# A four-layer kernel on one core: its last phase in another order, and layernorm statistics aggregated by fours

## The chip, the core and the metric

The kernel runs on one core of a Trainium2 chip. The core has five engines with instruction streams of their own: TensorE (PE) for matmuls, VectorE (DVE), ScalarE (ACT) and GpSimd (POOL) for elementwise work, and SyncE (SP), which here issues the DMAs. They wait for one another through semaphores. PE's matmuls write to PSUM, and the other engines empty PSUM into SBUF. The metric is the time on the device in microseconds (us), as the median of several runs.

## The reference

The input is x of 4 batches with 1024 tokens of 256 numbers, all float32. Four layers follow one another, each added to its input:

```python
x = x + attention(layernorm(x))   # one head, causal softmax, no output product
x = x + mix(layernorm(x))
x = x + state(layernorm(x))
x = x + mix(layernorm(x))         # the same weights as above

def mix(x):                       # x_prev: the token before, zero ahead of the first
    xr = mu_r * x + (1 - mu_r) * x_prev
    xk = mu_k * x + (1 - mu_k) * x_prev
    return sigmoid(xr @ W_r.T) * (square(relu(xk @ W_k.T)) @ W_v.T)

def state(x):
    xn = (x - mean) / sqrt(var + 1e-5) * ln_g + ln_b
    x_proj, z = split(xn @ W_in.T + b_in, 2)
    z = silu(z)
    y = conv(x_proj @ W_B.T * mean(dt)) @ W_C.T + D_skip * x_proj
    return (y * z) @ W_out.T + b_out + x
```

The convolution runs along the tokens of a batch, with 16 channels, each with a kernel of averaged powers of its decay.

## The kernel before, in words

The tokens of a batch are worked in two halves of 512; half j is half j % 2 of batch j // 2, so there are eight, 0 to 7. The names of tiles carry the layer and the half: a is the attention's normalization, f the first mix, h the state layer, g the second mix, whose result is the output. A tile with features on the partitions and tokens along the row is 128x512, and a half has two of them (e = 0, 1); a tile with tokens on the partitions is 128x256, and a half has four of them.

**The work of one half in a layer.** `normalized` (L584) makes the statistics of four tiles of rows: bn_stats (L622) and bn_aggr (L623) of each on DVE, then the variance ve (L648), its power −1/2 rs on POOL (L661), the shift mrs (L670), and the normalized rows xn on DVE (L676, L688) or ACT. For the second mix some halves are done with sums on ACT instead. `by_dram` (L731) turns them: rows_ is written to memory and read back as blocks_ by four DMAs, all on SP's queue, and DVE transposes the blocks (L750) into hT. The mix shifts it into xk and xr (L974 on ACT, L977 on DVE). Then come, on PE, keys (p.gks, L858, or pk, L793 where a half is done alone), gates pr (L928, the sigmoid of it is r) and values pv (L928); ka (L1038, L1047) is the squared relu of the keys, r is multiplied by the values on DVE (L1095), and the sum with x is made on POOL (L1101).

**Products by seven.** For a whole batch, `seven_products` (L840) makes a product of 2x2 blocks with seven block products instead of eight. The units on PE are called p1, p2, p6, p5, p7, p4, p3. Sums T1 to T4 of the input's halves are made ahead (`stream_sums`, L832) on POOL or DVE; three of the intermediate products are copied out of PSUM as u (L783 on ACT, L784 on DVE); and DVE combines these with the products held in PSUM (L905, L907) into the four results c11, c22, c21, c12. The keys of mix 2 (gks), the gates of the state layer (zs), its skip path (ss) and the attention's queries (qs) of most batches go this way.

**The state layer.** z is the gate, skip the skip path, `mix_states` (L1942) makes py = states times W_C on PE, adds it to skip (L1961 on DVE) and multiplies z by that (L1965, on POOL or DVE). `state_outputs` (L1982) is the product pyo with W_out, and DVE adds it to x (L1989). `convolve` (L1856) needs the inputs of all four batches, so the layer has a meeting point: gates and skip paths can come before or after it, outputs only after it.

**What sets the order.** A planner, `Order` (L54), gets the work as units for PE in the order in which the program calls them, and as operations with one or more ways to do each (engine and cost in us, for instance POOL 1.05 or DVE). It computes when each is due, places them in a list schedule, with 20 plans and some rounds for each, and emits the plan that ends first by its own costs. PE's units keep the order of the calls, except that of the next few one that is ready may go ahead; which engine makes an operation, and when, is the planner's choice and depends on all costs. PSUM is a ring of four bank buffers and two pairs.

**The last phase** (from L2131) is a list of calls written out by hand: `more_gates(n)` issues the next n pieces of gates and skip paths of the state layer, `mix_states(b)` one batch's mixing, `outputs(j)` (L2127) a half's state output and the preparation of its second mix, `both(mix2.gates, j)` the gate of the second mix, `keys_of_batch(b)` with `advance(keys, n)` n of a batch's seven key units, `both(mix2.values, j)` the values.

Of the kernel before, what the change touches and what calls it, by code (L numbers as in the profile page):

```python
# [14 lines left out]
AF = mybir.ActivationFunctionType  # L15
ALU = mybir.AluOpType
# [13 lines left out]
HALF = 512  # L30
# [329 lines left out]
def dve(n):  # L360
    return 0.02 + n / 850


def act(n):
    return 0.22 + n * 0.72e-3
# [3 lines left out]
def hybrid_kernel(  # L369
# [34 lines left out]
    nc = tc.nc  # L404
    E = mybir.EngineType
    ctx.enter_context(tc.manual_schedule(engines={E.PE, E.Activation, E.DVE, E.Pool, E.SP}))
    o = Order()
# [120 lines left out]
    for j in range(4, 2 * NB):  # L528
        b, h = divmod(j, 2)
# [23 lines left out]
    for i in range(NB * NT):  # L553
        j = i // NH
# [29 lines left out]
    def normalized(  # L584
        key, b, h, needs, dst, names, second=False, by_hand=False, spans=((0, NH),),
        by_scalar=False,
# [11 lines left out]
        st = lazy(lambda: tiny(f"st_{key}", NH, 6))  # L598
        mv = lazy(lambda: tiny(f"mv_{key}", NH, 2))
# [20 lines left out]

        def stats(n):
            nc.vector.bn_stats(st()[:, n, :], row(n))  # L622
            nc.vector.bn_aggr(mv()[:, n, :], st()[:, n, :])  # L623

        def sums(n):
            nc.scalar.activation(
# [66 lines left out]
        if by_scalar:  # L693
            for n in range(NH):
                o.op(f"{key}.su{n}", [needs[n]], ("ACT", act(D) + 0.11, partial(sums, n)))
            o.op(f"{key}.me", [f"{key}.su{n}" for n in range(NH)], ("POOL", 0.2, means))
            for n in range(NH):
                o.op(f"{key}.st{n}", [f"{key}.me"], ("ACT", act(D) + 0.11, partial(squares, n)))
            variances_of = lambda n0, n1: by_sums()
            shifts_of = lambda n0, n1: shifts_by_sums()  # L700
        else:
            for n in range(NH):
                o.op(f"{key}.st{n}", [needs[n]], ("DVE", 0.53, partial(stats, n)))
            variances_of, shifts_of = variances, shifts
        for n0, n1 in spans:
            span = "" if n1 - n0 == NH else f"{n0}"
            some = range(n0, n1)
            o.op(
                f"{key}.ve{span}", [f"{key}.st{n}" for n in some],
                ("DVE+port", 0.08 * k, partial(variances_of, n0, n1)),  # L710
            )
            o.op(
                f"{key}.rs{span}", [f"{key}.ve{span}"],
                ("POOL", 0.4 + 0.62 * k, partial(powers, n0, n1)),
            )
            o.op(
                f"{key}.mrs{span}", [f"{key}.rs{span}"],
                ("DVE+port", 0.08 * k, partial(shifts_of, n0, n1)),
            )
            for n in some:  # L720
                o.op(
                    f"{key}.xn{n}", [f"{key}.mrs{span}"],
                    ("DVE+port", dve(D), partial(on_vector_by_sums if by_scalar else on_vector, n)),
                    ("ACT", act(D) + 0.1, partial(on_scalar, n)),
                )
# [89 lines left out]
    def stream_sums(key, src, needs):  # L815

        t = [lazy(lambda k=k: cols(f"T{k}_{key}")) for k in range(KC)]

        def b(c, h):
            return src(h)[:, c, :]  # L820

        def sums(k):
            return t[(k - 1) // 2]()[:, (k - 1) % 2, :]

        for k, plus, minus in (
            (1, lambda: b(0, 1), lambda: b(0, 0)),
            (3, lambda: b(1, 1), lambda: b(0, 1)),
            (2, lambda: b(1, 1), lambda: sums(1)),
            (4, lambda: b(1, 0), lambda: sums(2)),
        ):  # L830
            def emit(engine, k=k, plus=plus, minus=minus):
                engine.tensor_sub(sums(k), plus(), minus())  # L832

            o.op(
                f"{key}.T{k}", needs + ([f"{key}.T{k - 1}"] if k in (2, 4) else []),
                ("POOL", 1.05, partial(emit, nc.gpsimd)), ("DVE+port", dve(HALF), partial(emit, nc.vector)),
            )
        return sums

# [103 lines left out]

    class Mix:
        def __init__(self, tag, needs, last):
            self.tag, self.needs, self.last = tag, needs, last
# [52 lines left out]
        def keys(self, j, e):  # L1001
            key = f"{self.tag}{j}"
            if e == 0:
                self.ka[j] = lazy(lambda: cols(f"ka_{key}"))
            ka = self.ka[j]
            pk = project_columns(
                f"{key}.pk{e}", w_fk, e, self.xk[j], [f"{key}.xk{c}" for c in range(KC)] + ["w_f"]
            )
            o.op(
                f"{key}.relu{e}", [f"{key}.pk{e}"],  # L1010
                ("ACT", act(HALF), lambda: nc.scalar.activation(ka()[:, e, :], pk(), AF.Relu)),
                ("DVE", dve(HALF), lambda: nc.vector.tensor_scalar_max(ka()[:, e, :], pk(), 0.0)),
                frees="bank",
            )
            o.op(
                f"{key}.ka{e}", [f"{key}.relu{e}"],
                ("POOL", 1.05, lambda: nc.gpsimd.tensor_mul(ka()[:, e, :], ka()[:, e, :], ka()[:, e, :])),
                ("ACT", act(HALF), lambda: nc.scalar.square(ka()[:, e, :], ka()[:, e, :])),
            )

        def keys_of_batch(self, b):

            js = (2 * b, 2 * b + 1)
            key = f"{self.tag}ks{b}"
            there = [f"{self.tag}{j}.xk{c}" for j in js for c in range(KC)]
            for j in js:
                self.ka[j] = lazy(lambda j=j: cols(f"ka_{self.tag}{j}"))
            ka, xk = [self.ka[j] for j in js], [self.xk[j] for j in js]

            def src(h):  # L1030
                return xk[h]()

            def by_scalar(t):
                nc.scalar.activation(t(), t(), AF.Relu)
                nc.scalar.square(t(), t())

            def by_vector(t):
                nc.vector.scalar_tensor_tensor(t(), t(), 0.0, t(), ALU.max, ALU.mult)  # L1038

            T = stream_sums(key, src, there)  # L1040
            o.op(f"{self.tag}{js[0]}.ka1", [f"{key}.c21"], ("none", 0.0, lambda: None), lag=0.0)
            out = lambda e, h: ka[h]()[:, e, :]

            def direct(e, h, p):
                def emit():
                    nc.scalar.activation(out(e, h), p(), AF.Relu)
                    nc.scalar.square(out(e, h), out(e, h))  # L1047

                return (("ACT", 2 * act(HALF), emit),)

            for e, h in ((0, 0), (1, 1), (0, 1)):
                t = lambda e=e, h=h: ka[h]()[:, e, :]
                o.op(
                    f"{self.tag}{js[h]}.ka{e}", [f"{key}.c{e + 1}{h + 1}"],
                    ("ACT", 2 * act(HALF), partial(by_scalar, t)),
                    ("DVE+port", dve(HALF), partial(by_vector, t)),
                )
            return seven_products(
                key, key, fk_block, lambda k: fk_sums[:, k - 1, :], src, T,
                added(out), direct, ["fk_sums", "w_f"], there,  # L1060
            )

# [879 lines left out]
    def mix_states(b):  # L1942
# [25 lines left out]
        for h in range(2):  # L1968
            j = 2 * b + h
            for e in range(KC):  # L1970
                o.op(
                    f"g{e}.{j}", [f"pm{b}", f"ss{b}.c{e + 1}{h + 1}"],
                    ("DVE", dve(HALF) + 0.03, partial(grown, j, e)),
                    frees="bank",
                )
                o.op(
                    f"y{e}.{j}", [f"g{e}.{j}", f"z{e}.{j}"],
                    ("POOL", 1.05, partial(gated, nc.gpsimd, j, e)),
                    ("DVE+port", dve(HALF), partial(gated, nc.vector, j, e)),
                )  # L1980

# [18 lines left out]
    def both(unit, j):  # L2000
        unit(j, 0)
        unit(j, 1)
# [115 lines left out]
    def more_gates(n):  # L2118

        for _ in range(n):  # L2120
            next(all_gates)

    def advance(chain, n):
        for _ in range(n):
            next(chain)

    def outputs(j):  # L2127
        both(state_outputs, j)
        mix2.prepare(j)
# [37 lines left out]
    mix_states(0)  # L2167
    more_gates(8)
    outputs(0)
    more_gates(5)  # L2170
    mix_states(1)
    outputs(1)
    more_gates(4)
    outputs(2)
    more_gates(4)
    mix_states(2)
    outputs(3)
    more_gates(3)
    keys = mix2.keys_of_batch(0)
    both(mix2.gates, 0)  # L2180
    outputs(4)
    advance(keys, 2)
    outputs(5)
    advance(keys, 2)
    more_gates(3)
    advance(keys, 3)
    both(mix2.gates, 1)
    mix_states(3)
    both(mix2.values, 0)
    both(mix2.values, 1)  # L2190
    outputs(6)
    keys = mix2.keys_of_batch(1)
    both(mix2.gates, 2)
    outputs(7)
    advance(keys, 7)
    both(mix2.gates, 3)
    both(mix2.values, 2)
    keys = mix2.keys_of_batch(2)
# [66 lines left out]
```

## Time and profile before

| | |
|---|---|
| median of 3 runs | 464.14 us (464.13 to 464.68) |
| the profiled execution | 464.18 us |
| its span, from the first to the last instruction | 462.4 us |
| mean granted TensorE clock | 1.000 |
| instructions in the span | 6630 |
| DMA | 69.44 MB, 149 GB/s over the span |

The span is cut into 40 slices on the page of the profile, and each digit is the busy share in tenths:

```profile
PE   8999999999999999999999999999999999999996
DVE  4898697989989888788989977425689989998852
ACT  3322334453284453554335755523467887743452
POOL 3001002303032412332221568512255216336240
```

A slice is 11.6 us. The attention and the first mix fill the first 24 slices or so, the meeting point of the state layer lies at slices 24 to 27, where DVE and POOL have little to do, and the outputs and the second mix fill the rest. A row of the timeline gives the start, the duration, the engine and line, the operation with its output and inputs, and the idle time before it with what ended it. Ends of matmuls are modelled: the distance from one group's start to the next one's is the better measure.

### The profile page before, as it was taken

What the parts mean: (1) busy time and instruction counts of PE and PEld (TensorE: products, weight loads), DVE (VectorE), ACT (ScalarE), POOL (GpSimd) and SP (SyncE); (2) the same over time, 40 slices, a digit from 0 to 9 for tenths busy, and PEclk for the clock granted to TensorE, in tenths of its full rate; (3) what the DMA queues carried; (4) which work ended last, traced back from release to release, by engine and by line L of the source; (5) the groups of instructions that cost most, each with busy time, mean ns of one, the idle gap of its engine ahead of it and who ended that gap; (6) DMA issues with size and microseconds to landing.
All of it is one profiled execution on the core that took longest, in us unless ns stands there. A gap on an engine that the chain in (4) does not pass through costs nothing.

```text
span 462.4 us, 6630 instructions
## 1 busy us (share of the span) xinstructions
PE 454.6 (98%) x2052; PEld 311.4 (67%) x2052; DVE 370.7 (80%) x914; ACT 227.0 (49%) x473; POOL 139.4 (30%) x145
## 2 busy tenths in 40 slices
PE   8999999999999999999999999999999999999996
PEld 5665776667786767776678774473565857686675
DVE  4898697989989888788989977425689989998852
ACT  3322334453284453554335755523467887743452
POOL 3001002303032412332221568512255216336240
PEclk9999999999999999999999999999999999999999
DMA  8067958684358641428784869503014042604522
GB/s 236 27 170 209 272 143 236 169 252 151 101 160 213 184 138 51 137 87 256 226 261 128 276 220 276 213 15 90 13 63 121 0 143 86 215 14 135 178 75 68
DMA packets 84915, 69.44 MB, mean 150 GB/s; under 512 B 20160, under 2 KB 82576, under 8 KB 84880
## 3 DMA queue, kind: packets, MB, share of 16 engines
q1 hardware_dynamic: 84064, 68.76, 50.2%
q8 instruction: 16, 0.26, 0.2%
q10 hardware_dynamic: 816, 0.26, 0.2%
q14 instruction: 19, 0.16, 0.1%
HBM read 40.54 MB, written 28.45 MB: 149 GB/s over the span
## 4 chain that ended last, share of the span: by engine, by line
PE 84%; DVE 10%; POOL 3%; issue 1%; SPq 1%; DMA 1%; ACT 0%; DVEq 0%; POOLq 0%
PE po L1655 14%; PE sc L1550 13%; PE pv L1522 6%; PE held_zs L858 3%; PE held_ss L858 3%; PE held_qs L858 2%; PE held_gks L858 2%; PE pc L1862 2%; PE dust L1339 1%; DVE T_gks L832 1%; DVE xr_g L977 1%; DVE xk_g L977 1%; POOL x L1101 1%; PE pp_a0.pq L793 1%; PE pp_g6.pk L793 1%
## 5 line engine op out<-in xcount | busy, mean ns | idle before, releaser
L1655 PE MATMUL po<-v,prT 128*128 128x256 f32 x288 | 67.6, 380 | 0.0
L1550 PE MATMUL sc<-xa,q 128*128 128x512 f32 (+3 forms) x192 | 66.9, 486 | 0.0
L1655 PEld LDWEIGHTS po<-v,prT 128*128 128x128 f32 x288 | 54.2, 189 | 11.6 <-issue 3.1
L1571 ACT ACTIVATE pr<-pr,nmx 128x128 f32<-128x128 f32 (+7 forms) x32 | 24.7, 773 | 69.7 <-DVE pr L1566 57.1
L1550 PEld LDWEIGHTS sc<-xa,q 128*128 128x128 f32 x192 | 34.8, 190 | 24.3 <-issue 20.1
L1522 PE MATMUL pv<-wv,xa 128*128 128x257 f32 x128 | 32.7, 380 | 0.0
L1101 POOL TENSOR_TENSOR x<-x,r_f 128x512 f32<-128x512 f32 x16 | 20.8, 1298 | 35.7 <-DVE r_f L1095 33.8
L1522 PEld LDWEIGHTS pv<-wv,xa 128*128 128x128 f32 x128 | 23.9, 191 | 8.4 <-issue 4.1
L1608 DVE STREAM_TRANSPOSE prT<-pblocks 128x384 f32<-128x384 f32 (+7 forms) x30 | 24.0, 798 | 4.8 <-DMA pblocks<-exps 4.8
L661 POOL TENSOR_TENSOR rs_h<-ve_h,minus_half 128x8 f32<-128x8 f32 x8 | 13.2, 1646 | 47.9 <-DVE ve_h L650 47.9
L1566 DVE TENSOR_SCALAR_CACHE_REDUCE pr<-sc,v 128x128 f32<-128x128 f32 (+7 forms) x32 | 26.2, 818 | 1.1
L661 POOL TENSOR_TENSOR rs_a<-ve_a,minus_half 128x4 f32<-128x4 f32 x7 | 7.4, 1060 | 62.8 <-DVE ve_a L648 52.9
L1101 POOL TENSOR_TENSOR x<-x,r_g 128x512 f32<-128x512 f32 x14 | 20.1, 1446 | 16.8 <-DVE r_g L1095 16.8
L1699 POOL TENSOR_TENSOR x<-x,bout_r 128x512 f32<-128x512 f32 x16 | 20.7, 1302 | 13.3 <-ACT x L1692 9.8
L1692 ACT ACTIVATE x<-x,mrs_h,rs 128x256 f32<-128x256 f32 x32 | 17.2, 588 | 6.5 <-DVE rs L1703 6.5
L1965 POOL TENSOR_TENSOR z<-z,skip 128x512 f32<-128x512 f32 x11 | 15.0, 1384 | 17.4 <-DVE skip L1961 17.3
L661 POOL TENSOR_TENSOR rs_f<-ve_f,minus_half 128x4 f32<-128x4 f32 x8 | 8.1, 1016 | 39.2 <-DVE ve_f L648 34.1
L1664 DVE SCALAR_TENSOR_TENSOR x<-po,rsm,x 128x256 f32<-128x256 f32 x32 | 14.9, 467 | 5.4 <-PE po L1655 5.3
L622 DVE BATCH_NORM_STATS2 st_a<-x 128x6 f32<-128x256 f32 x32 | 13.0, 407 | 3.0 <-DMA x<-in_L_attn_a_X_dram 3.0
L974 ACT ACTIVATE xk_g<-hT_g,muk 128x512 f32<-128x512 f32 x16 | 11.0, 713 | 8.4 <-DVE hT_g L750 8.4
L1532 DVE TENSOR_TENSOR v<-pv,bv_r 128x257 f32<-128x257 f32 x32 | 13.2, 413 | 2.2 <-PE pv L1522 1.8
L977 DVE SCALAR_TENSOR_TENSOR xr_g<-hT_g,mur,xr_g 128x512 f32<-128x512 f32 x16 | 14.4, 920 | 0.5 <-ACT xr_g L974 0.5
(478 smaller groups left out, 1070.3 us busy)
## 6 DMA issues: line engine op xcount, KB each, us to landing
hk<-r_dram SPq DMA_DIRECT2D x16, 512.0 KB, 6.6
rows_g<-xn_g SPq DMA_DIRECT2D x8, 512.0 KB, 3.0
blocks_g<-rows_g SPq DMA_DIRECT2D x32, 128.0 KB, 2.7
x<-in_L_attn_a_X_dram SPq DMA_DIRECT2D x7, 512.0 KB, 5.1
rows_f<-xn_f SPq DMA_DIRECT2D x7, 512.0 KB, 3.5
blocks_f<-rows_f SPq DMA_DIRECT2D x28, 128.0 KB, 2.7
rows_h<-xn_h SPq DMA_DIRECT2D x7, 512.0 KB, 3.3
blocks_h<-rows_h SPq DMA_DIRECT2D x28, 128.0 KB, 2.9
```

Of the source, the lines that this page charges most:

```text
L661: nc.gpsimd.tensor_tensor(rs()[:, :k].rearrange("p k n -> p (k n)"), ve()[:, :k].rearrange("p k n -> p (k n)"), minus_half[:, : k * NH], A ...
L858: lambda: nc.tensor.matmul(dst(), lhsT=w(), rhs=data(), start=first, stop=True, skip_group_check=True),
L977: nc.vector.scalar_tensor_tensor(t()[:, c, :], hT()[:, c, :HALF], mu1[:, c : c + 1], t()[:, c, :], ALU.mult, ALU.add,)
L1101: nc.gpsimd.tensor_add(xg, xg, r()[:, ts(g, 2), :])
L1522: nc.tensor.matmul(pv()[:, : D + 1], lhsT=xaj()[:, c, ts(n, P)], rhs=wv[:, c, :], start=(c == 0), stop=(c == KC - 1),)
L1550: nc.tensor.matmul(sc()[:, k * HALF : k * HALF + w], lhsT=qh()[:, c, ts(n, P)], rhs=keys[k]()[:, c, :w], start=(c == 0), stop=(c == KC - 1),)
L1566: nc.vector.tensor_scalar(dst, src, v[2 * b + h]()[:, n, D : D + 1], None, ALU.add, ALU.min, accum_out=nmx(),)
L1571: nc.scalar.activation(p()[:, :nk], p()[:, :nk], AF.Exp, bias=nmx(), scale=-1.0, accum_out=sm())
L1608: nc.vector.transpose(dst()[:, : NH * width].rearrange("p (k m a) -> p k m a", m=NH, a=GRP), blocks().rearrange("p m (k a) -> p k m a", a= ...
L1655: nc.tensor.matmul(po()[:, :D], lhsT=src()[:, ts(n, P)], rhs=v[2 * b + n // NH]()[:, n % NH, :D], start=(n == 0), stop=(n == t),)
L1692: nc.scalar.activation(xt, xt, AF.Identity, bias=mrs()[:, 0, n : n + 1], scale=rs1()[:, n : n + 1])
L1699: nc.gpsimd.tensor_add(xg, xg, bout_r.unsqueeze(1).to_broadcast([P, 2, D]))
```

## The change

It has four parts.

- The operation on a tile's statistics held bn_stats and bn_aggr; now bn_stats alone is in it, and a new operation, `ag`, does the aggregates of a group of rows (four, or the part of them that a span names) when all their statistics are there.
- The planner's cost of a POOL multiply or sum of 128x512 goes from 1.05 to 1.25 in three places: the sums T, the squares ka of a half done alone, and the z products.
- The two ways of a squared relu of the keys of a batch move to a helper, `squares`. The instructions are the same, the costs given to the planner are 1.13 and 0.03 more.
- The calls of the last phase stand in another order: outputs of halves 1 to 3 and the mixing of batches 1 and 2 come between fewer pieces of the gates; the key units of batch 0 alternate with the remaining gates one by one; outputs(5) comes after these; the mixing of batch 3 comes after the gates of half 2; values(1) and outputs(6), outputs(7) come in between the key units of batch 1.

```diff
@@ normalized
         def stats(n):
             nc.vector.bn_stats(st()[:, n, :], row(n))
-            nc.vector.bn_aggr(mv()[:, n, :], st()[:, n, :])
+
+        def gather(n0, n1):
+            for n in range(n0, n1):
+                nc.vector.bn_aggr(mv()[:, n, :], st()[:, n, :])
...
             for n in range(NH):
-                o.op(f"{key}.st{n}", [needs[n]], ("DVE", 0.53, partial(stats, n)))
+                o.op(f"{key}.st{n}", [needs[n]], ("DVE", 0.36, partial(stats, n)))
...
+            made = [f"{key}.st{n}" for n in some]
+            if not by_scalar:
+                o.op(
+                    f"{key}.ag{span}", made,
+                    ("DVE", 0.06 + 0.1 * (n1 - n0), partial(gather, n0, n1)),
+                )
+                made = [f"{key}.ag{span}"]
             o.op(
-                f"{key}.ve{span}", [f"{key}.st{n}" for n in some],
+                f"{key}.ve{span}", made,
...
@@ stream_sums
-                ("POOL", 1.05, partial(emit, nc.gpsimd)), ("DVE+port", dve(HALF), partial(emit, nc.vector)),
+                ("POOL", 1.25, partial(emit, nc.gpsimd)), ("DVE+port", dve(HALF), partial(emit, nc.vector)),
@@ Mix
+    def squares(dst, src, port=""):
+
+        def by_scalar():
+            nc.scalar.activation(dst(), src(), AF.Relu)
+            nc.scalar.square(dst(), dst())
+
+        def by_vector():
+            nc.vector.scalar_tensor_tensor(dst(), src(), 0.0, src(), ALU.max, ALU.mult)
+
+        return ("ACT", 1.13, by_scalar), ("DVE" + port, dve(HALF) + 0.03, by_vector)
...
@@ Mix.keys
-                ("POOL", 1.05, lambda: nc.gpsimd.tensor_mul(ka()[:, e, :], ka()[:, e, :], ka()[:, e, :])),
+                ("POOL", 1.25, lambda: nc.gpsimd.tensor_mul(ka()[:, e, :], ka()[:, e, :], ka()[:, e, :])),
@@ mix_states
-                    ("POOL", 1.05, partial(gated, nc.gpsimd, j, e)),
+                    ("POOL", 1.25, partial(gated, nc.gpsimd, j, e)),
@@ the last phase, from L2167
     mix_states(0)
     more_gates(8)
     outputs(0)
-    more_gates(5)
+    more_gates(2)
     mix_states(1)
+    more_gates(2)
     outputs(1)
-    more_gates(4)
+    more_gates(1)
     outputs(2)
-    more_gates(4)
+    more_gates(2)
+    outputs(3)
+    more_gates(2)
     mix_states(2)
-    outputs(3)
-    more_gates(3)
     keys = mix2.keys_of_batch(0)
     both(mix2.gates, 0)
+    advance(keys, 2)
+    more_gates(2)
     outputs(4)
-    advance(keys, 2)
+    for _ in range(5):
+        advance(keys, 1)
+        more_gates(1)
+    both(mix2.gates, 1)
     outputs(5)
-    advance(keys, 2)
     more_gates(3)
-    advance(keys, 3)
-    both(mix2.gates, 1)
-    mix_states(3)
     both(mix2.values, 0)
-    both(mix2.values, 1)
-    outputs(6)
     keys = mix2.keys_of_batch(1)
     both(mix2.gates, 2)
+    mix_states(3)
+    both(mix2.values, 1)
+    advance(keys, 4)
+    outputs(6)
+    advance(keys, 3)
     outputs(7)
-    advance(keys, 7)
     both(mix2.gates, 3)
     both(mix2.values, 2)
```

More of the change, by code (lines that the diff above doesn't have):

```diff
@@ L1031, in src @@
                 return xk[h]()
[L1033 to L1038, printed above, removed]
             T = stream_sums(key, src, there)
@@ L1044, in direct @@
             def direct(e, h, p):
[L1045 to L1049, printed above, removed]
+                return squares(lambda: out(e, h), p)[:1]
             for e, h in ((0, 0), (1, 1), (0, 1)):
@@ L1054, in keys_of_batch @@
                     f"{self.tag}{js[h]}.ka{e}", [f"{key}.c{e + 1}{h + 1}"],
-                    ("ACT", 2 * act(HALF), partial(by_scalar, t)),
-                    ("DVE+port", dve(HALF), partial(by_vector, t)),
+                    *squares(t, t, "+port"),
                 )
```

## The prediction, written before the changed kernel was run

> **What bounds the kernel now.** I read the busy table first, then what TensorE waits for, then busy time by stretch of the last phase, then the timelines of the stretches with a wait.
>
> ```profile
> PE 454.6 (98%) x2052; PEld 311.4 (67%) x2052; DVE 370.7 (80%) x914; ACT 227.0 (49%) x473; POOL 139.4 (30%) x145
> ```
>
> TensorE (PE) is busy for 98% of the span of 462.4 us. Matmuls are the same 1077 before and after, in another order, so the time changes only by what TensorE waits. Its waits (total, times, longest, in us):
>
> ```profile
> PE dust L1339 <- DVE idle L446: 1.2, 1, 1.2
> PE pr_g4.pv L928 <- ACT ka_g L1047: 0.9, 1, 0.9
> PE held_gks L858 <- DVE u_gks L784: 0.9, 1, 0.9
> PE held_zs L858 <- DVE z L907: 0.6, 1, 0.6
> PE pt_h7.T L775 <- DVE xn_h L676: 0.3, 1, 0.3
> ```
>
> The first is the start and isn't touched. The other four lie where the change works. I size them from start to start: sixteen 256-wide matmuls take 3.45 us (g2.pv starts at 408.49, the next group at 411.94), so 0.216 each, and a 512-wide one 0.43. In the timelines (start, duration, instruction, idle time before it):
>
> ```profile
> 324.14 1.02 PE L858 MATMUL held_ss<-xnT,wk 128*128 128x512 f32 x2
> 324.95 0.75 DVE L907 SCALAR_TENSOR_TENSOR z<-held_zs,b_all,u_zs 128x512 f32<-128x512 f32 x1
> 325.75 1.13 PE L858 MATMUL held_zs<-T_zs,w_in 128*128 128x512 f32 x2 [0.59 <-DVE z L907]
> ```
>
> Two 512-wide matmuls end at 324.14 + 0.86 = 325.0 and the next starts at 325.75: 0.75 lost to a buffer that DVE empties late.
>
> ```profile
> 422.36 1.89 PE L928 MATMUL pr_g5.pr<-w_r,xr_g 128*128 128x256 f32 x8
> 422.76 1.27 POOL L1101 TENSOR_TENSOR x<-x,r_g 128x512 f32<-128x512 f32 x1
> 422.82 1.23 DVE L670 SCALAR_TENSOR_TENSOR mrs_g<-rs_g,mv_g 128x4 f32<-128x4 f32 x1 [0.54 <-POOL rs_g L661]
> 424.29 0.68 DVE L784 COPY u_gks<-held_gks 128x512 f32<-128x512 f32 x1
> 425.12 1.10 PE L858 MATMUL held_gks<-T_gks,fk_sums 128*128 128x512 f32 x2 [0.86 <-DVE u_gks L784]
> 428.31 0.15 DVE L670 SCALAR_TENSOR_TENSOR mrs_g<-rs_g,mv_g 128x4 f32<-128x4 f32 x1
> 429.60 0.59 PE L928 MATMUL pr_g4.pv<-w_fv,ka_g 128*128 128x256 f32 x2
> 430.43 0.63 ACT L1047 ACTIVATE ka_g<-ka_g 128x512 f32<-128x512 f32 x1
> 431.12 1.13 PE L928 MATMUL pr_g4.pv<-w_fv,ka_g 128*128 128x256 f32 x4 [0.92 <-ACT ka_g L1047]
> ```
>
> g5.pr takes 425.12 − 422.36 = 2.76 for 1.73 of work: 1.03 lost to a copy of a product (u_gks) that stands on DVE behind mrs_g. g4.pv's third matmul comes 1.52 after its first where two take 0.43: 1.09 lost to the last square of batch 2's keys. pt_h7.T loses 0.64: the products before it stand 2.21 for 1.85, the transposes 1.15 for 0.87. Together 0.64 + 0.75 + 1.03 + 1.09 = 3.51.
>
> By stretch (window; length; busy PE, PEld, DVE, ACT, POOL; clock; DMA share; GB/s):
>
> ```profile
> 320.00:350.00 30.00, 29.41 (x103) 16.65 (x103) 21.91 (x37) 16.26 (x50) 12.09 (x12) 1.00 0.17 53
> 388.00:422.00 34.00, 34.00 (x139) 24.56 (x138) 33.66 (x66) 17.42 (x30) 15.14 (x12) 1.00 0.34 109
> ```
>
> From 388 to 422 DVE is full (33.66 of 34), and the chain that ended last runs on DVE there: this is the place where DVE sets the end. In 320–350 it has 8.1 us idle, in 350–388 some 2.8: 10.9 in all. The granted clock is 1.00.
>
> **The change part by part.** Places come from the changed program's instruction order per engine, priced with rows of before.
>
> *Statistics by fours.* Each bn_aggr (0.18) now follows its group's four bn_stats (0.41) instead of its own one. The variance waited for all four anyway, and the same eight instructions run. The pair in turn takes 0.53, so a group 2.13; side by side between 2.13 and 1.8 (no chained start). I take zero: until 240 us xk and xn are ready 6 to 17 us ahead of TensorE, which hides it. Without that cover one group would gain up to 0.33.
>
> *Costs of POOL's multiplies at 1.25.* They run nothing; they steer who does what. Five z products go from POOL to DVE, and three key sums T_gks net; DVE has 892 instructions for 884, POOL 143 for 150. All u_gks and u_zs copies go to ACT, three u_ss copies come to DVE.
>
> ```profile
> L1965 POOL TENSOR_TENSOR z<-z,skip 128x512 f32<-128x512 f32 x11 | 15.0, 1384 | 17.4 <-DVE skip L1961 17.3
> L1965 DVE TENSOR_TENSOR z<-z,skip 128x512 f32<-128x512 f32 x5 | 4.0, 830 | 0.0
> ```
>
> With DVE's 512-wide products at 0.60 to 0.66 start to start, DVE's work from the first skip to the end is 106.6 us instead of 102.6, and up to the second half of xr_g5 86.1 instead of 78.2 (7.9 more, part of it work that stood behind xr_g5). The 10.9 us idle ahead can take this up if the inputs come early, which the order does.
>
> *The order.* On TensorE pyo.3 comes 6.2 us earlier, pyo.4 4.3, g0.pr 5.15, the keys of batch 0 4.3, pyo.5 7.75 later. All four waits named go:
> - pt_h7.T stands 2.57 later, behind three products of the gates; and h6's rows leave SP's queue ahead of h5's. xn_h7 is there at about 288.8, the transposes' place is 290.1. Gone 0.64.
> - z of that unit stands one operation earlier on DVE: ready at about 324.2, needed at 325.0. Gone 0.75.
> - u_gks is on ACT, not behind mrs_g. Gone 1.03.
> - eight matmuls of g5.pr (1.73) now stand ahead of g4.pv and cover the 1.09. Gone 1.09.
>
> New waits by the same walk:
> - u_zs of batch 1 on ACT behind a gate's activation and two products: 0.25 (bounds 0 and one ACT operation, 0.63).
> - u_ss of batch 3 on DVE behind an xn and the state output's addition: unit 6 of ss3 waits 0.6 (bounds 0 and 1.3, two such operations).
> - g5.pr needs xr_g5's second half. From the last state output on, DVE needs a product that TensorE gives 12.27 later; then one subtraction 0.66, mrs_g6 1.15, three xn 1.0, xr 0.66: 15.74, where TensorE comes at 14.85. Wait 0.9. Its mrs_g6 I price as in the row above (1.23, stretched while POOL adds; mrs_g7 took 0.15): unstretched the wait is −0.1, so 0. Upward: if four more of POOL's five additions there each stretch a DVE operation by 1.0 (two did before, by 1.07 and 0.95), less 1.24 of cover, the wait is 0.9 + 2.8 = 3.7. I take 0.9, as the trace of before has few such hits.
>
> On SP the four loads of xmT_3 move between the blocks and rows of g0 and g1 (about 0.6 of issue each, 2.4 ahead of rows_g1), and output stores between rows of g6 and its blocks; xk_g1 is due 1.0 before the keys, so up to 1.4 if that were all late, but rows_g1 itself is some 4 earlier. ACT's silu table load now stands ahead of r_f7's sigmoid; ACT is idle there.
>
> A rule to weigh: the Trainium skill, page "SBUF — State Buffer", section "Who interferes with whom", says that VectorE and GpSimd share a port pair as an exclusive lock and that the loser blocks for the whole instruction. The row of mrs_g (1.23 for 0.15) agrees in size. By the rule, as an estimate, five POOL additions of 1.27 ahead of xr_g5 could block 6.4 us, less 1.24 of cover: a wait of about 5 and a time near 466.5; it speaks against moving work to DVE beside POOL.
>
> By the rows, two of the seven POOL operations of 411–424 caught a DVE operation (mrs_g 1.07, T_gks 0.95 longer), far fewer than the rule would allow.
>
> Sum: −3.51 + 0.25 + 0.6 + 0.9 = −1.76. Against the profiled execution's 464.18 that is 462.4; the median of the runs, 464.14, stands 0.04 below it.
>
> **The rivals.**
> 1. *All waits go and none comes*: xr_g5 in time because no stretch falls on it. 464.18 − 3.51 = 460.7, up to 461.6 with half of the new. For it: unstretched, xr_g5 needs only 0.1 less; against: DVE is full.
> 2. *Exchange*: the 7.9 us more of DVE up to xr_g5 aren't taken up by the idle time ahead, because the idle time is waiting for pyo. Then xr_g5, which before was done at 417.84, comes at 425.7, its place is 422.65, a wait of 3.1: 464.18 − 3.51 + 0.85 + 3.1 = 464.6, no change.
> 3. *Slower, at g0.pr.* g0.pr moves ahead 5.15 and the waits gone before it 1.39, while its input may not.
>
> ```profile
> 353.77 2.98 DVE L977 SCALAR_TENSOR_TENSOR xr_g<-hT_g,mur,xr_g 128x512 f32<-128x512 f32 x2 [0.20 <-ACT xr_g L974]
> ...
> 357.65 2.54 PE L928 MATMUL pr_g0.pr<-w_r,xr_g 128*128 128x256 f32 x11
> ```
>
> xr_g0 was done at 356.75, 0.9 ahead of use at 357.65. If it stays there, TensorE at 351.3 waits 5.4: 464.18 − 3.51 + 0.25 + 5.4 = 466.3. It decides from a wait over 4.2, xr_g0 later than about 355.6. Against it: the first half's additions and statistics now stand ahead of other work, and through the round trip by memory (7.2) I find xr_g0 ready at 349.7, 1.5 before its place.
>
> 4. *It doesn't do what it says*: if aggregates side by side cost as much as in turn and the cost figure moves nothing that matters, only the order counts; that is inside the forecast, since I gave them zero.
>
> **How the numbers follow.** What a measurement of this kernel tells from no change is about 0.2%, 0.93 us: faster is under 463.2, slower over 465.1. Forecast (461.6 to 463.2) 0.42; all waits go 0.15; exchange and what else ends within 0.2% 0.21; slower, by g0.pr, by the 3.7 at xr_g5 (464.18 − 3.51 + 0.85 + 3.7 = 465.2), or by a mixture, 0.22. Faster is 0.42 + 0.15 = 0.57. The range runs from rival 1 (460.7, no lower since no more waits are there) to just under rival 3, 466.0, leaving out about 0.05 below and 0.12 above. The forecast's own range is 461.6 to 463.2.
>
> **What would show it.** After, the list of waits lacks pt_h7.T, held_zs in batch 2, u_gks before g5.pr, and ka_g before g4.pv; a wait of g5.pr for xr_g of about 0.9 and of held_ss for u_ss of about 0.6 are new. DVE is full from g3.pr to g5.pr. xr_g0 is done before 352. Wrong is the forecast if g0.pr waits for xr_g, if g5.pr waits over 2 us (DVE bound), if a POOL operation stretches several DVE operations of 400–422, or if TensorE waits somewhere before 280, where the replanned other engines might be late though I counted 6 us and more of slack.

## The result, and the profile after

The changed kernel takes 469.62 us in the median of six runs (468.43 to 470.3), the kernel before 464.55 (464.13 to 465.43): a ratio of 1.0102, with a 95% interval from 1.0083 to 1.0122. It is slower by 5.1 us; 462.4 was forecast, and 460.7 to 466.0 as the range. The profiled execution took 469.5 us, its span is 467.7.

The busy table and the longest waits of TensorE in the changed kernel (total, times, longest, in us):

```profile
PE 457.2 (98%) x2052; PEld 312.9 (67%) x2052; DVE 366.3 (78%) x922; ACT 227.4 (49%) x473; POOL 131.3 (28%) x138
```

```profile
PE held_gks L868 <- ACT u_gks L793: 2.8, 1, 2.8
PE dust L1348 <- DVE idle L446: 1.2, 1, 1.2
PE pt_h7.T L785 <- DVE xn_h L679: 0.8, 1, 0.8
PE pr_g4.pr L938 <- DVE r_g L1104: 0.7, 1, 0.7
PE pr_g0.pr L938 <- DVE skip L1970: 0.4, 1, 0.4
```

Of the four old waits two are gone (held_zs for z, g4.pv for ka_g), two are back in a larger form. Taken from start to start, TensorE lost some 5.2 us more than before, and the span grew by 5.3 (467.7 for 462.4): that is the whole result. By place, in this profile: 1.3 more between 200 and 310 (the transposes of h7 and what follows them), 0.2 more between 310 and 405, 3.3 more from 405 on, 0.4 in the first 200. The largest piece, TensorE's timeline of the changed kernel:

```profile
423.58 1.96 PE L868 MATMUL held_gks<-T_gks,fk_sums 128*128 128x512 f32 x4
428.33 1.28 PE L868 MATMUL held_gks<-T_gks,fk_sums 128*128 128x512 f32 x2 [2.79 <-ACT u_gks L793]
429.40 3.46 PE L938 MATMUL pr_g5.pr<-w_r,xr_g 128*128 128x256 f32 x8
```

Unit 7 of batch 2's keys (p7) waits 2.8 us for u2, the second of the three products that are copied out of PSUM. Behind it the eight matmuls of g5.pr take 3.30 until the next start instead of 1.73. Busy time by stretch of the same kernel (PE, PEld, DVE, ACT, POOL, then clock, DMA share, GB/s) shows why:

```profile
400.00:413.00 13.00, 13.00 (x58) 10.70 (x57) 10.16 (x19) 6.40 (x11) 1.51 (x2) 1.00 0.40 122
413.00:432.00 19.00, 15.52 (x55) 10.65 (x54) 18.58 (x40) 7.06 (x12) 6.97 (x7) 0.93 0.25 83
...
425.00:429.40 4.40, 1.61 (x4) 0.48 (x3) 4.40 (x10) 2.16 (x4) 2.15 (x3) 0.97 0.06 21
429.40:432.70 3.30, 3.30 (x9) 2.65 (x8) 2.30 (x10) 0.66 (x2) 0.72 (x1) 0.52 0.75 250
```

The granted clock is 0.52 in 429.4 to 432.7: half speed, straight after the wait. That is part of the loss, not all of it: the one run whose mean clock of 0.999 leaves no room for such a stretch (3.4 us at half speed take 0.004 off the mean) took 468.48, still 3.9 above before. And VectorE, idle for 2.8 us in 400 to 413, is full from 413 to 432 (18.58 of 19). The copy itself, in the timelines of VectorE and ScalarE:

```profile
425.95 1.22 DVE L673 SCALAR_TENSOR_TENSOR mrs_g<-rs_g,mv_g 128x4 f32<-128x4 f32 x1
427.21 0.60 ACT L685 ACTIVATE xn_g<-x,mrs_g,rs_g 128x256 f32<-128x256 f32 x1 [3.20 <-DVE mrs_g L673]
427.71 0.56 ACT L793 COPY u_gks<-held_gks 128x512 f32<-128x512 f32 x1
```

u2 has moved from VectorE to ScalarE, but ahead of the copy ScalarE's list has a row xn_g6, which stood waiting for the same mrs_g6 for 3.20 us, and the copy started only behind it. mrs_g6 comes at 425.95, where it came at 422.82 before. Following the chain back, VectorE had waited for a transfer:

```profile
403.72 0.50 ACT xn_g L685
404.23 4.86 DMA rows_g<-xn_g
...
410.45 2.58 DMA blocks_g<-rows_g
413.05 1.31 DVE hT_g L760 x2
```

hT_g5 starts at 413.05, 5.7 us later than in the kernel before, whose timeline has

```profile
407.35 0.70 DVE L750 STREAM_TRANSPOSE hT_g<-blocks_g 128x512 f32<-128x512 f32 x1
```

and VectorE's work for half 5 comes in one heap. The runs below show that a late hT_g5 does not make the loss by itself: it starts at 413.19 in e7 and 412.97 in e18, where nothing waits for u2, and at 408.76 in e12, which has the whole loss.

### The profile page after: what moved, and what is told of

Read it like the earlier page. It is cut to its first block, busy times and chain, and to the rows that moved or that the text cites. A ratio compares the mean times of both kernels' runs of the same rounds, so it can differ in the third digit from the quotient of the medians.

```text
span 467.7 us, 6600 instructions
## 1 busy us (share of the span) xinstructions
PE 457.2 (98%) x2052; PEld 312.9 (67%) x2052; DVE 366.3 (78%) x922; ACT 227.4 (49%) x473; POOL 131.3 (28%) x138
## 4 chain that ended last, share of the span: by engine, by line
PE 83%; DVE 9%; DMA 3%; ACT 2%; issue 1%; SPq 1%; POOL 0%; DVEq 0%
PE po L1664 13%; PE sc L1559 13%; PE pv L1531 6%; PE held_ss L868 3%; PE held_qs L868 2%; PE held_gks L868 2%; PE held_zs L868 2%; DMA rows_g<-xn_g 2%; PE pc L1871 2%; DMA blocks_g<-rows_g 1%; PE dust L1348 1%; PE pr_g5.pr L938 1%; PE pp_a0.pq L803 1%; DVE xk_g L998 1%; PE pr_f7.pr L938 1%
## 5 line engine op out<-in xcount | busy, mean ns | idle before, releaser
L1569 DVE TENSOR_TENSOR sc<-sc,mask 128x128 f32<-128x128 f32 x32 | 9.3, 290 | 10.5 <-PE sc L1559 10.2
L995 ACT ACTIVATE xk_f<-hT_f,muk 128x512 f32<-128x512 f32 x16 | 10.9, 716 | 12.2 <-DVE hT_f L760 12.1
L664 POOL TENSOR_TENSOR rs_g<-ve_g,minus_half 128x4 f32<-128x4 f32 x8 | 9.4, 1180 | 20.6 <-DVE ve_g L643 13.9
```

Source lines behind the costliest of these rows:

```text
L664: nc.gpsimd.tensor_tensor(rs()[:, :k].rearrange("p k n -> p (k n)"), ve()[:, :k].rearrange("p k n -> p (k n)"), minus_half[:, : k * NH], A ...
L995: nc.scalar.mul(t()[:, c, :], hT()[:, c, 1:], mu[:, c : c + 1])
```

## The experiments

In "plan kept" kernels the planner's finished list is taken as it is, and single entries are moved or given another engine; every other instruction keeps its place. In "planned anew" kernels the program is edited and the planner runs again. Times before, in the same comparisons, were 464.3 to 464.6.

### The copy, xr_g5, and both (changed kernel, plan kept)

```diff
 plan, self.due = chosen
 self._run(plan, True)
 ...
+self._move('gks2.u2', ahead='g6.mrs')   # e1 and e3
+self._move('g5.xr0', ahead='g6.mrs')    # e2 and e3
```

> The changed kernel with one instruction moved: the copy u2 of batch 2's keys (u_gks on ScalarE) stands ahead of the normalized row xn_g6 that waits for mrs_g6, not behind it. Theory 1, two late things stand one behind the other: the copy (on ScalarE) and xr_g5's second half (on VectorE, behind mrs_g6 and three rows of xn_g6, ready at about 428.8). Then unit 7 starts at about 425.4 instead of 428.33, and g5.pr waits instead until 428.8, where it now starts at 429.4: gain 0.6, 468.9; if the shorter wait also spares TensorE's clock drop (1.5), 467.4. Rival: the copy's place alone made the loss: 2.8 and the 1.5 behind it go, 465.2.

Measured: 469.03 (468.07 to 470.72), ratio 1.0098 (1.0074 to 1.0121). That is near theory 1's 468.9 and far from the rival's 465.2, but the clock stayed at 1.00 in this profile, and for that case theory 1 gave 467.4. TensorE's timeline shows the wait split in two:

```profile
427.61 1.13 PE L884 MATMUL held_gks<-T_gks,fk_sums 128*128 128x512 f32 x2 [0.67 <-ACT u_gks L809]
430.35 1.97 PE L954 MATMUL pr_g5.pr<-w_r,xr_g 128*128 128x256 f32 x8 [1.61 <-DVE xr_g L1014]
```

> The changed kernel with one instruction moved: xr_g5's second half on VectorE ahead of mrs_g6. Theory 1: mrs_g6 and with it the copy on ScalarE come later by one operation, 0.7: unit 7 waits 3.5 instead of 2.8, time 469.5 + 0.7 = 470.2, and g5.pr waits for nothing. Rival, VectorE's order alone makes the loss: 466 to 468.

Measured: 471.77 (470.72 to 472.84), ratio 1.0153 (1.0131 to 1.0174): slower than the changed kernel, as theory 1 says, but by 2.2 instead of 0.7. The wait for the copy is 3.4 us, 0.6 longer, and g5.pr waits for nothing, both as theory 1 has it:

```profile
431.75 1.13 PE L884 MATMUL held_gks<-T_gks,fk_sums 128*128 128x512 f32 x2 [3.39 <-ACT u_gks L809]
```

> Both moves, the copy ahead of xn_g6 on ScalarE and xr_g5's second half ahead of mrs_g6 on VectorE. Theory 1: unit 7 starts at about 425.4, g5.pr at about 426.6 to 427.3 instead of 429.4, and the wait is too short for the clock drop: 469.5 - 2.5 - 1.5 = 465.5. The gain is larger than those of the two single moves added. Rival, VectorE is simply full from 417 on: the wait moves on to unit 4 or g4.pv and less than 1.5 is gained.

Measured: 468.21 (467.65 to 469.84), ratio 1.0072 (1.0055 to 1.0089). The forecast of 465.5 is missed; the rival holds (1.4 gained). In its profile, which is of the slowest of its runs, TensorE waits 0.68, 0.51 and then, new, ahead of unit 4:

```profile
428.33 1.12 PE L885 MATMUL held_gks<-T_gks,fk_sums 128*128 128x512 f32 x2 [0.68 <-ACT u_gks L810]
429.97 1.97 PE L955 MATMUL pr_g5.pr<-w_r,xr_g 128*128 128x256 f32 x8 [0.51 <-DVE mrs_g L690]
432.96 1.12 PE L885 MATMUL held_gks<-T_gks,w_fk 128*128 128x512 f32 x2 [1.03 <-DVE ka_g L932]
```

So in these three runs the wait, taken away in one place, comes back one unit on: I read it as the place where the load of VectorE shows, and not as what makes the loss.

The whole times hide a part of this. TensorE starts g4.pr, ahead of everything that was edited, at 417.45 in the changed kernel's profile and at 419.03, 420.53 and 420.15 in e1 to e3: in these profiles the transposes of h7 lose 1.1 more, and e3 has its half clock at 294. From there to the start of g4.pv the changed kernel takes 18.70 us and e1 to e3 take 16.63, 17.35 and 16.36. So at the place itself e1 gained 2.1 and e3 2.3, but some 1.6 of it is the half clock that none of the three has there. What the moves took from the waits is some 0.5 in e1 and 0.7 in e3; e2 lost some 0.2.

### The clock (changed kernel, plan kept)

```diff
+self.todo.insert(self._place('gks2.p7'), ('fill', 'PE', self.fill))
 ...
+                for _ in range(6):
+                    nc.tensor.matmul(
+                        pr()[:, 0, :], lhsT=ident, rhs=w[:, 0, :], start=True, stop=True,
+                        skip_group_check=True,
+                    )
```

> The changed kernel with six matmuls of 0.43 us added on TensorE in front of unit 7 of batch 2's keys, where it waits for 2.8 us; their result is overwritten by g5.pr. Nothing else is moved and the wait for the copy stays. If the granted clock of 0.52 in 429.4 to 432.7 comes from TensorE having stood still before, it stays near 1.0 and g5.pr takes 1.73 instead of 3.3: 469.5 - 1.5 = 468.0. If the clock falls for another reason, or the stretch is slow for lack of data, the time stays 469.5.

Measured: 469.51 (469.04 to 470.2), ratio 1.0105 (1.009 to 1.012). Not decided by the time: in its profile the clock is 1.00 in 430 to 434 and g5.pr takes 1.73 there, but the clock is 0.55 in 294.4 to 297.9 instead, behind two waits of 0.73 and 0.94 at the transposes. And e1 and e2 had the clock at 1.00 there without the added matmuls. That the stretch is slow for lack of data is out, since the profile shows the clock itself. The last section counts over all profiles what stood ahead of the half clock.

### GpSimd beside xn_h7 (changed kernel, plan kept)

```diff
+# in normalized, for h7; listed behind the last row of xn_h7
+o.late = lambda: nc.gpsimd.tensor_copy(ve()[:, 0, 0:2], xn()[:, 3, 0:2])
```

> The changed kernel, its plan kept, with one 128x2 copy added on GpSimd that reads the last VectorE row of xn_h7: GpSimd's additions of the state layer's bias can no longer run beside mrs_h7 and xn_h7. If the stretch of these four VectorE operations beside GpSimd (1.23 for 0.15, 1.38 and 1.35 for 0.4) makes TensorE wait at the transposes of h7 (1.0 to 2.1 from run to run), they take 0.15 and 0.4 and that wait goes: 469.4 - 1 to 2 = 467.4 to 468.4. If what the transposes wait for is the later r_f7 and its additions, xn_h7 starts just as late and less than 0.4 is gained.

Measured: 467.92 (466.04 to 468.19), ratio 1.0068 (1.0047 to 1.009): 1.7 less than the changed kernel in the median, as the first theory says. The wait of 2.8 for u2, and in the profile the half clock behind it, stay. VectorE and GpSimd in the changed kernel, and then VectorE in this one:

```profile
287.79 1.30 DVE L673 SCALAR_TENSOR_TENSOR mrs_h<-rs_h,mv_h 128x4 f32<-128x4 f32 x2
289.02 3.21 DVE L679 TENSOR_SCALAR xn_h<-x,mv_h,rs_h 128x256 f32<-128x256 f32 x3
287.73 2.52 POOL L1708 TENSOR_TENSOR x<-x,bout_r 128x512 f32<-128x512 f32 x2
290.77 2.59 POOL L1708 TENSOR_TENSOR x<-x,bout_r 128x512 f32<-128x512 f32 x2
```

```profile
287.61 0.24 DVE L689 SCALAR_TENSOR_TENSOR mrs_h<-rs_h,mv_h 128x4 f32<-128x4 f32 x2
287.76 1.05 DVE L695 TENSOR_SCALAR xn_h<-x,mv_h,rs_h 128x256 f32<-128x256 f32 x3
```

The same five operations take 0.24 + 1.05 alone and 1.30 + 3.21 beside GpSimd's additions, 3.2 us more, and the transposes no longer wait.

### The order, the statistics and the costs, each alone (planned anew)

```diff
 # e6: the changed kernel with the last phase's calls of before
 # e7: the kernel before with the new calls
 # e12: the kernel before with the new costs
 # e13: the kernel before with the statistics by fours
```

> The changed kernel with the calls of the last phase in the order of before; statistics by fours and the new costs stay (12 of the 16 z products are then on VectorE, even more than in the changed kernel). Theory A, the order of the calls makes the loss, since outputs(5) comes late and batch 2's second half reaches VectorE in one heap: without it the time is that of before within 0.4%, 462.5 to 466. Theory B, the work moved from GpSimd to VectorE makes it: 468 to 470.

> The kernel before with the calls of the last phase in the new order and nothing else of the change (costs and statistics as before). Theory A (the order): 468 to 470, hT_g5 some 5 us later than before and VectorE full behind it. Theory B (the work moved by the costs): 463 to 465.

> The kernel before with the new costs (1.25 for GpSimd, and those of the squares) alone: order of calls and statistics as before. The costs and the statistics together gave 468.4 with the old order. If the work that the costs move to VectorE makes that loss: 467.5 to 469. If the statistics make it: 464 to 465.

> The kernel before with the statistics aggregated by fours alone. If the costs make the loss of 4 us and the statistics are worth nothing, as I forecast: 464 to 465. If the statistics make it (the aggregates at the end of a group stand behind other work on VectorE, and the whole plan changes): 467 to 468.5.

| what of the change is in | median us | ratio to before, 95% |
|---|---|---|
| statistics (e13) | 464.92 | 1.0008 (0.9998 to 1.0017) |
| order (e7) | 466.25 | 1.0047 (1.0032 to 1.0062) |
| costs (e12) | 469.91 | 1.0116 (1.0098 to 1.0134) |
| statistics and costs (e6) | 468.37 | 1.0092 (1.0071 to 1.0112) |
| all | 469.62 | 1.0102 (1.0083 to 1.0122) |

The statistics are worth nothing that can be measured. The order alone costs 1.9; its own wait is another one (held_zs for a copy on ScalarE, 1.5 at 353) and it does cut the losses after 405, by about 1. The costs alone make as much as the whole change. So theory A, which I held after the first runs, falls: with the old order the loss stays. (By its profile e6 has 8 of the 16 z products on VectorE, not the 12 expected; the changed kernel has 10.) In e12 the copy u2 is on VectorE, and TensorE waits for it just as long:

```profile
PE held_gks L858 <- DVE u_gks L784: 2.8, 1, 2.8
PE pr_g3.pr L928 <- DVE skip L1960: 1.2, 1, 1.2
```

### outputs(5) earlier (planned anew), and two sums back on GpSimd (plan kept)

```diff
     outputs(4)
+    outputs(5)
     for _ in range(5):
         advance(keys, 1)
         more_gates(1)
     both(mix2.gates, 1)
-    outputs(5)
```

> The changed kernel with one call moved: outputs(5) straight behind outputs(4) instead of behind the key units of batch 0 and the gates of half 1. Theory A: hT_g5 is some 5 us earlier, VectorE has work in its idle 2.9 us of 400 to 413, the copy that unit 7 waited 2.8 us for comes in time, 464.5 to 466. Rival: VectorE has too much to do from 388 on wherever outputs(5) stands, 467.5 to 470.

Measured: 469.06 (468.35 to 470.26), ratio 1.011 (1.0092 to 1.0127): the rival holds. hT_g5 comes only 1.4 earlier, at 411.7, and the wait for u2 is still 2.0.

```diff
+self._to('gks2.T3', 'POOL')
+self._to('gks2.T4', 'POOL')
```

> The changed kernel, its plan kept, with two of batch 2's key sums, T3 and T4, put on GpSimd again (before, two of the four were there). If VectorE's work in 413 to 432 sets the end, its 1.38 ahead of mrs_g6 is saved and the copy behind it comes that much sooner: 469.4 - 1.4 = 468.0, 467.5 at best. If more GpSimd work there only stretches what VectorE does beside it: 469 to 470.

Measured: 471.14 (469.56 to 472.25), ratio 1.0143 (1.0113 to 1.0172), slower still; the second theory holds. What VectorE saves (1.38) comes back as stretches beside GpSimd: a sum beside T3, xr_g5 beside an addition, mrs_g6 beside T4 (426.92 to 428.18), and three rows of xn_g6 beside the addition that follows at 428.18. GpSimd's T3 and VectorE's rows in this kernel:

```profile
418.19 1.71 POOL L859 TENSOR_TENSOR T_gks<-xk_g 128x512 f32<-128x512 f32 x1 [0.63 <-DVE xk_g L1015]
```

```profile
418.81 1.64 DVE L859 TENSOR_TENSOR T_gks<-xk_g,xk_g 128x512 f32<-128x512 f32 x1
423.61 1.30 DVE L1015 SCALAR_TENSOR_TENSOR xr_g<-hT_g,mur,xr_g 128x512 f32<-128x512 f32 x1
427.02 1.18 DVE L690 SCALAR_TENSOR_TENSOR mrs_g<-rs_g,mv_g 128x4 f32<-128x4 f32 x1
428.12 2.12 DVE L696 TENSOR_SCALAR xn_g<-x,mv_g,rs_g 128x256 f32<-128x256 f32 x3
```

In the changed kernel the first two took 0.69 and 0.73, mrs_g6 1.22 (1.18 here), and the three rows 1.04. So this edit of one stretch doesn't tell the load of VectorE from its neighbour; the next runs put the question the other way round, in the plan of before.

### The moved work inside the plan of before (plan kept)

```diff
+self._to('gks2.T3', 'DVE')                # e14 and e16
+self._to('gks2.T4', 'DVE')
+for h in range(6):                        # e15 and e16
+    self._to(f'y1.{h}', 'DVE')
+self._to('y0.7', 'POOL')
```

> The kernel before, its plan kept, with the key sums T3 and T4 of batch 2 on VectorE instead of GpSimd, as the changed kernel has them. Theory V (work moved to VectorE in a stretch where it is full): two operations of 0.6 to 0.7 stand ahead of mrs_g6, and the copy behind it that TensorE waits 1.0 for comes 1.3 later: 464.5 + 1.3 = 465.8. Theory P (the moved work is harmless in itself, what costs is the whole other plan that the planner makes with these costs): 464.2 to 464.8.

Measured: 467.08 (466.33 to 467.29), ratio 1.0061 (1.0045 to 1.0078), 2.7 more. Theory V, with a larger price: in the profile (466.33) the wait for u2, 0.9 before, is

```profile
PE held_gks L875 <- DVE u_gks L801: 2.4, 1, 2.4
```

> The kernel before, its plan kept, with the z products as the changed kernel has them: second ones of halves 0 to 5 on VectorE, the first of half 7 on GpSimd. Six moved operations lie in 320 to 388, where VectorE had 10.9 us idle, so both theories expect little; V: 464.5 to 465.3, P: 464.2 to 464.8. If skip and z on VectorE delay the outputs behind them: 466 and more.

Measured: 465.5 (465.16 to 466.34), ratio 1.0029 (1.0017 to 1.004), 1.2 more.

> Both moves in the plan of before. V: 465.8 to 466.6. P: 464.2 to 465.

Measured: 467.9 (467.11 to 469.58), ratio 1.0087 (1.0061 to 1.0112), 3.6 more, above V's 466.6. Its profile, of the slowest of its four runs (469.58), has the picture of the changed kernel, a wait of 2.8 for u2 and half the clock behind it:

```profile
PE held_gks L878 <- DVE u_gks L804: 2.8, 1, 2.8
```

```profile
429.50:432.90 3.40, 3.40 (x9) 2.70 (x8) 2.80 (x6) 0.00 (x0) 0.48 (x1) 0.51 0.48 161
```

### Each cost alone (planned anew)

```diff
 # e17: stream_sums, e18: mix_states
-("POOL", 1.05, ...
+("POOL", 1.25, ...
 # e19: the squares' costs
```

> The kernel before with the cost 1.25 for the key and gate sums T alone, planned anew. All new costs together gave 469.9. If the sums on VectorE around 410 to 425 make that: 468 to 470. If the z products make it: 464 to 465.5.

> The kernel before with the cost 1.25 for the z products alone, planned anew. The cost of the sums T alone changed nothing (0.9992), all new costs together gave 469.9. If the z products on VectorE (10 or so of 16 instead of 5) make that: 467 to 470. If it takes several of the costs together: 464 to 465.5.

> The kernel before with the new costs of the squares alone (1.13 and 0.03 more, GpSimd's 1.25), planned anew. If the squares' costs send copies and squares to other engines at the batch 2 crossing and make the loss: 467 to 470. If not: 464 to 465.5.

Measured: 463.74, ratio 0.9992 (0.9978 to 1.0006); 465.31, 1.0017 (1.0007 to 1.0026); 464.45, 1.0002 (0.9988 to 1.0015). No single cost makes the loss. e17 has all four sums of batch 2 on VectorE, which cost 2.7 in the plan of before, and loses nothing, because its plan also puts u2 on ScalarE in time (a wait of 0.5). e18 has 8 of the 16 z products on VectorE instead of 5 and loses 0.9. Together they give the plan that is 5.4 slower; two of the three together were not run. Why the planner takes that one for the best by its own costs was not tried.

### The waits of before, taken away one by one (kernel before, plan kept)

```diff
+self.todo.insert(self._place('h7.xn3') + 1, ('late', 'POOL', self.late))  # the copy of e5
+self._move('y0.1', behind='zs2.c22')
+self._to('gks2.u2', 'ACT')
+self._move('gks2.u2', ahead='g4.ka0')
+self._to('gks2.u3', 'ACT')
+self._move('g4.pr1', ahead='g5.pr1')
+self._move('gks2.p7', ahead='g6.xn1')
+self._move('gks2.u3', behind='gks2.p7')
+self._move('g4.g1', behind='g4.pr1')
+self._move('g5.pr1', behind='gks2.p4')
+self._move('gks2.c21', ahead='g5.pr1')
```

> The kernel before with its plan kept and the four waits of its trace attacked by moving single instructions: a 128x2 copy on GpSimd that waits for the last row xn_h7 holds back the additions that stretched mrs_h7 (0.64 at pt_h7.T); the product z of batch 0's second half stands behind z_5 on VectorE (0.75); the copies u2 and u3 of batch 2's keys are on ScalarE ahead of the xn_g6 rows (1.03); g4.pr's second half stands between units 7 and 4, g5.pr's second half and the first square between units 4 and 3 (1.09). If the waits are what they seem: 464.2 - 3.5 = 460.7. If VectorE's load sets the end and the waits only show where it does: 463.5 to 464.5.

Measured: 462.07 (461.99 to 462.42), ratio 0.9952 (0.9937 to 0.9967): 2.3 faster than before and 7.5 faster than the changed kernel, the best of all. All four waits are gone from its list; apart from the one at the start only these are in it:

```profile
PE pp_g6.pk L821 <- DVE xk_g L1005: 0.6, 1, 0.6
PE held_gks L886 <- DVE ka_g L933: 0.4, 1, 0.4
```

The expected 460.7 is missed by 1.4; these two new waits, 1.0 together, are the part of it that the list shows.

## Why the prediction was wrong, point by point

**What bounds the kernel.** Right: the matmuls are the same, and the result is what TensorE waits.

**Statistics at zero.** Right: 1.0008 alone.

**The costs of GpSimd's multiplies, "they run nothing".** This is the step that failed first: the costs alone lose 5.4 (e12). I counted the moved work (7.9 us more up to xr_g5) and then let the 10.9 us of VectorE's idle time take it up. Inside the plan of before, two moved sums and the z products cost 3.6 us (e16); the idle time lay elsewhere, or was waiting for inputs. In the changed kernel VectorE is idle 2.8 in 400 to 413 and full behind it. How much of the changed kernel's 5.1 is this load and how much is the rest of its other plan stays open: e17 moves the sums too, in a plan of its own, and loses nothing.

**"u_gks is on ACT, not behind mrs_g. Gone 1.03."** Wrong, and the largest single miss: on ScalarE it stands behind xn_g6, which waits for mrs_g6. I looked at the engine of the copy and not at what is queued ahead of it. The cover was gone too: before, eight matmuls of g5.pr stood between units 5 and 6 and unit 7; now unit 7 follows at once. Instead of −1.03 the place costs 3.1 and 1.6 for the clock.

**The wait of g5.pr for xr_g5, 0.9.** The walk took it that VectorE is ready when TensorE gives the product p2 of batch 2. It was not: p2 was there at 423.58, and VectorE came to it at 425.36. Ahead of that lie 1.6 of idle time for blocks_g5 and 1.7 of two stretches beside GpSimd's additions (xk_g5's second half 1.77 for 0.74, T1_gks2 1.38 for 0.69). The first of these is one of the three in the first row:

```profile
414.85 3.08 DVE L998 SCALAR_TENSOR_TENSOR xk_g<-hT_g,muk,xk_g 128x512 f32<-128x512 f32 x3
420.49 1.38 DVE L842 TENSOR_TENSOR T_gks<-xk_g 128x512 f32<-128x512 f32 x1
425.36 0.67 DVE L915 TENSOR_TENSOR ka_g<-p_gks,u_gks 128x512 f32<-128x512 f32 x1
```

The wait is hidden behind that for u2; with the copy moved ahead it shows as 1.6 (e1). The bound of 3.7, which I gave for this place as an end, was nearer than the value I took.

**pt_h7.T, 0.64 gone.** Wrong: I had xn_h7 ready at 288.8; it was ready at 292.2, since mrs_h7 and the rows of xn_h7 ran beside GpSimd's additions. With the additions held back (e5) the last of these rows ends at 288.8, the number counted. These additions stand in slices 24 and 25 (counted from 0) of the profile, where GpSimd's digits of before are 8 and 5: that it has little to do at 24 to 27 holds for the last two only.

**held_zs, 0.75 gone, and g4.pv, 1.09 gone.** Right, both. **u_zs1 0.25 and u_ss3 0.6**: about 0.3 and 0.35. The first is right by luck: the copy on ScalarE was done at 301.34, and what TensorE waited for was z on VectorE (301.67 to 302.41), behind a sum T_zs that took 1.52.

**The rivals.** g0.pr had its input in time: xr_g0 was done at 352.94, later than my 349.7, and TensorE waited 0.57 there, for skip and not for xr_g0. The exchange came nearest in mechanism, VectorE late by about 3 us at batch 2, but I kept all four gains beside it. Not foreseen were 0.96 at g4.pr, where r_g2 on VectorE (419.30 to 419.98) frees the PSUM buffer of g2.pv late, and the clock.

**The rule on the port pair.** I weighed the Trainium skill, "SBUF — State Buffer", section "Who interferes with whom", against two hits in seven rows and took the rows. The count of two left out the other side: in the same rows of before GpSimd's T_gks took 1.77 and three additions 4.73, where a single one takes 1.27 in two other rows, so GpSimd was probably held up as well. The row is now 3.21 for 1.05 (three rows of xn_h7, e5). The rule that the loser blocks for the whole instruction, and that tensor_scalar is among the operations that can contend, agrees with it.

## What to carry to other kernels

A copy that moves to another engine takes its place in that engine's queue: what stands ahead of it there, and what that waits for, decides whether it comes sooner. Idle time of a nearly full engine counts as room only if the moved work's inputs are there in it. Where a planner makes the order, a changed cost is a changed plan: hold the plan fixed and move single operations to learn what an operation costs (here 2.3 us were gained that way).

## What the runs showed of the hardware

TensorE's clock fell to half for 3.41 us in the middle of seven of the profiles: starting at 427 to 430 in the changed kernel, e5, e12 and e16, at 422 in e6 and at 294 in e3 and e4. It cost 1.5 to 1.7 us each time. It doesn't come behind every long wait: e2 waited 3.4 with the clock at 1.00 behind it. Busy time and clock of the changed kernel, and then of e2:

```profile
425.76:429.17 3.41, 0.84 (x2) 0.48 (x3) 3.41 (x7) 1.93 (x4) 1.39 (x3) 1.00 0.01 3
429.17:432.58 3.41, 3.41 (x9) 2.54 (x8) 2.53 (x10) 0.89 (x2) 0.60 (x1) 0.50 0.77 259
```

```profile
426.93:430.34 3.41, 1.43 (x4) 0.36 (x2) 3.41 (x7) 0.00 (x0) 2.29 (x3) 1.00 0.18 59
430.34:433.75 3.41, 2.00 (x7) 1.42 (x8) 2.71 (x9) 2.81 (x5) 0.00 (x0) 1.00 0.35 120
```

In every profile the half clock starts a whole number of 3.41 us after the moment, 4 to 7 us into the span, at which the clock first stood at full. In stretches of 3.41 us laid out from there, and with matmuls counted at their usual distance, TensorE stood still for 2.79 (e5), 2.68 (changed kernel), 2.60 (e16), 2.54 (e6), 2.52 (e12), 2.17 (e4) and 2.10 us (e3) in the stretch just ahead of the half clock. The longest that it stood still in any other stretch inside the work are 2.15 (e2), 2.12 (e10) and 2.03 us (e9 and e10). e2's wait of 3.4 lies across two stretches, with 2.15 and 1.51. So, read from these profiles, a wait brings the half clock on when some 2.1 us or more of it fall into one such stretch (no closer than this count can tell), and where the stretches lie changes from run to run. No run moved a wait against them to test this.

The Trainium skill, "TensorE: Matmul & The Clock Gate", Part 1, gives half rate behind an idle window of about 3.4 us, in windows that run freely. The half rate, the length and the free windows agree; here waits shorter than a window were enough.

The runs of one kernel spread by it in part: e5 took 466.04 at a mean clock of 1.000 and 467.68 to 468.19 at 0.995 to 0.998, e10 469.56 at 1.000 and 472.0 to 472.3 at 0.993. But the changed kernel took 468.43 at 0.996 and 468.48 at 0.999, so there is another part to the spread.
